# Partition sums by 32x32 block transposes on VectorE, a 129th column of ones, wider first scores, a last pass on three engines

## The chip, the cores and the metric

The kernel runs on one core of a Trainium2 chip. A core has a matrix engine (TensorE, PE in the profile), three engines for elementwise work (VectorE or DVE, ScalarE or ACT, GpSimd or POOL), and SyncE (SP), which here only issues transfers from memory. Each engine takes its instructions strictly in the order in which they stand in the program, and waits for the others by semaphores. The metric is the device time of one execution in microseconds, the median of the runs shown.

## The reference: what is computed

Two cross-attention layers over a batch of 8; all numbers are float32. x has 100 rows of 1024 per batch, ctx has 1444 rows of 512.

Layer 0, per batch:

```python
Q = x @ Wq + bq;  K = ctx @ Wk + bk;  V = ctx @ Wv + bv      # hidden size 1024
weights = softmax(Q @ K.T * 1024**-0.5, axis=-1)             # over the 1444 context rows
x = x + (weights @ V) @ Wo + bo
```

Layer 1, per batch, on that x, with weights of its own:

```python
q = x @ Wq + bq;  k = ctx @ Wk + bk;  v = ctx @ Wv + bv
w = softmax(q @ k.T * 1024**-0.5, axis=1)                    # over the 100 rows of x
y = w @ v + x
out = (y - mean(y)) * rsqrt(var(y) + 1e-6) * gamma + beta    # over the 1024 columns
```

In layer 0 a row of weights sums to 1. In layer 1 it does not: the softmax runs over the other axis. So w @ (ctx @ Wv + bv) needs, for each row of x, the sum of its weights over the 1444 context rows, times bv.

## The kernel before, in words

The kernel never forms K and V. It multiplies weight matrices with each other first: Wq times Wk transposed (tile `qk0`, later `qk1`) and Wv times Wo (`vo0`), then folds x into the first (`queries`, tiles `g0T` and `g1T`), so that scores are g times ctx, and then only needs ctx itself.

**Stages in the order of time.** 
1. `weight_products("qk0")`, then `weight_products("vo0")`: 1024 x 512 and 512 x 1024 products by Strassen's scheme in seven half products on TensorE (helper `half_product`, L124, bank names x, z, y, w). VectorE makes the sums of blocks (L135) and adds partial products (L247), ScalarE copies others out of PSUM (L242). `accumulate` (L264, L266) makes on VectorE the products of a bias with the rows of a weight matrix: for each of 8 row blocks, times a column of the bias, added up. What is left is a sum over the 128 partitions.
2. `totals` (L301) makes that sum: it transposes 128x128 pieces through TensorE with the identity (L307) and reduces them from PSUM on VectorE (L308). It does so for `u0`, `wqbk0`, `bvo`, later `u1` and `wqbk1`: 20 transposes before `queries(0)` and 12 after `qk1`; the sums for `c0` add 8 more (L400, L401).
3. `queries(0)`: again seven products (`seven_products`, banks g_x, g_z, g_y, g_w). `left_sums` and `right_sums` are on VectorE (L135), `put` copies a bank out on ScalarE with the bias u (L353), `add` adds a bank on VectorE (L358). The order of products is X, Z, Y, X, X, W, Y: the second and third X product add into the banks of the first, with a `put` of those banks before each. `T_[2]`, the right sums of the third X product, is the tile `g_t3`. Between these copies ScalarE adds `out_bias` to xT, row block by row block (L406), in place; each waits until nobody else reads that row block of the old xT.
4. `key_bias_sums` (L329, L331) on VectorE, then `weight_products("qk1")`.
5. `scores0` of batches 0 and 1 alone (L488, 4 rows of blocks times 11 pieces of 131 or 132 columns in 4 banks), then eight passes that interleave `weighted_rows` of batch b (L458) with `scores0` of batch b + 2, matmul by matmul. Softmax runs on ScalarE and VectorE, the transposition of the probabilities on VectorE in 32x32 blocks (L523). For batches 0 and 7 the first four pieces are transposed on TensorE instead (`first_transposed`).
6. `project0`, `queries(1)`, and the same two-deep scheme for layer 1: `scores1` (L603) for batch b + 2 beside `attend1` (L659) for batch b. `weight_sums` (L639 to L641) adds the weights of a batch over its 12 pieces on VectorE; `weight_totals` (L647, L649) finishes the sum by a transpose on TensorE and a reduce. The result `r` is used at L731.
7. `finish`, `project_last`, `normalise`: residual, statistics, normalisation, stores. For the last batch the last multiply-add is done in two halves on VectorE (L754), one stored by SyncE and one by ScalarE.

**What sets the order.** TensorE's order is as written (`manual_schedule`). The order on VectorE, ScalarE and GpSimd is chosen when the program is built, and so is the choice of a PSUM bank (6 in one pool, 2 in the other). SyncE issues loads as written, each as soon as its buffer is free. ctx passes through ten buffers of one size (`unit`); a pass takes eight of them, four for rows (`load_rows`, tiles c, L437 and L441) and four for columns (tiles cT, L418 or L426).

Of the kernel before, what the change touches and what calls it, by code (L numbers as in the profile page):

```python
# [30 lines left out]
P = 128  # L31
# [10 lines left out]
CUTS = [S * n // NP for n in range(NP + 1)]  # L42
QD = 32
# [10 lines left out]
def two_layer_cross_attention(ctx: ExitStack, tc: tile.TileContext, a: dict, out: bass.AP):  # L54
# [17 lines left out]
    def unit(name):  # L72
        return stream.tile([P, E + L], F32, tag="unit", name=name)
# [113 lines left out]
    def weight_products(name, left, right, l_width, r_width, scaled):  # L187
# [10 lines left out]
        if name == "qk0":  # L198
            for part in (slice(0, lh // 2), slice(lh // 2, lh)):
                nc.scalar.dma_start(out=units[0][:, part], in_=lsrc[:, 0, part])  # L200
            nc.sync.dma_start(out=units[0][:, l_width : l_width + rh], in_=rsrc[:, 0, :rh])
            for h in range(1, EC):
                nc.sync.dma_start(out=units[h][:, :lh], in_=lsrc[:, h, :lh])
                nc.sync.dma_start(out=units[h][:, l_width:], in_=rsrc[:, h, :])
                if h == 1:
                    nc.sync.dma_start(out=units[0][:, l_width + rh :], in_=rsrc[:, 0, rh:])
            for i in range(H):
                for h in (i, H + i):
                    nc.sync.dma_start(out=units[h][:, lh:l_width], in_=lsrc[:, h, lh:])
        else:  # L210
            for h in range(EC):
                nc.sync.dma_start(out=units[h][:, :l_width], in_=lsrc[:, h, :])
                nc.sync.dma_start(out=units[h][:, l_width:], in_=rsrc[:, h, :])
# [37 lines left out]
        def accumulate(side):  # L251
            for v, of in scaled:
                if of != side:
                    continue
                width = (l_width, r_width)[side]
                if width == E:
                    acc = row(f"{name}_{v}")
                else:
                    acc = work.tile([P, L], F32, tag="half", name=f"{name}_{v}", bufs=1)
                accs[v] = acc  # L260
                for h in range(EC):
                    src = units[h][:, :l_width] if side == 0 else units[h][:, l_width:]
                    if h == 0:
                        nc.vector.tensor_scalar(acc, src, cols[v][:, h : h + 1], None, ALU.mult)  # L264
                    else:
                        nc.vector.scalar_tensor_tensor(acc, src, cols[v][:, h : h + 1], acc, ALU.mult, ALU.add)  # L266
# [33 lines left out]

    def totals(name, acc, n):  # L301

        got = const.tile([P, n], F32, tag=name, name=name)
        for c in range(0, n, 4):
            ps = bank(f"{name}_{c}")
            for i in range(4):
                nc.tensor.transpose(ps[:, i * P : (i + 1) * P], acc[:, (c + i) * P : (c + i + 1) * P], ident)  # L307
            nc.vector.tensor_reduce(got[:, c : c + 4], ps.rearrange("p (c q) -> p c q", q=P), AX.X, ALU.add)  # L308
        return got

    def bias_product(layer):

        prod = small.tile([P, EC], F32, tag="bb", name=f"bb{layer}")
        nc.vector.tensor_tensor(prod, cols[f"L{layer}_xattn_bq"], cols[f"L{layer}_xattn_bk"], ALU.mult)
        part = small.tile([P, 1], F32, tag="bbs", name=f"bbs{layer}")
        nc.vector.tensor_reduce(part, prod, AX.X, ALU.add)
        ps = bank(f"bb_ps{layer}")
        nc.tensor.matmul(ps[:, 0:1], ones, part, start=True, stop=True)
        got = const.tile([P, 1], F32, tag=f"bqbk{layer}", name=f"bqbk{layer}")
        nc.vector.tensor_scalar(got, ps[:, 0:1], SCALE, None, ALU.mult)  # L320
        return got

    def key_bias_sums(name, t0, t1, wqbk):

        acc = work.tile([P, GT], F32, tag="kb", name=name, bufs=3)
        for k in range(EC):
            src = xT[:, k, t0:t1]
            if k == 0:
                nc.vector.tensor_scalar(acc, src, wqbk[:, k : k + 1], None, ALU.mult)  # L329
            else:  # L330
                nc.vector.scalar_tensor_tensor(acc, src, wqbk[:, k : k + 1], acc, ALU.mult, ALU.add)  # L331
        return acc
# [52 lines left out]
    bqbk0 = bias_product(0)  # L385
    bqbk1 = bias_product(1)
    wvo, (acc_o,) = weight_products("vo0", "L0_xattn_WvT", "L0_xattn_Wo", L, E, (("L0_xattn_bv", 1),))
    u0 = totals("u0", acc_u, LC)
    wqbk0 = totals("wqbk0", acc_c, EC)
    nc.vector.tensor_tensor(out_bias, out_bias, totals("bvo", acc_o, EC), ALU.add)  # L390
    gT = [queries(0, wqk0, u0), None]
# [4 lines left out]
    c0 = const.tile([T, B], F32, tag="c0", name="c0")  # L396
    for g in range(B // G):
        ps = bank(f"c0_ps{g}")
        for i in range(G):
            nc.tensor.transpose(ps[:T, i * P : (i + 1) * P], kb0[g][:, i * T : (i + 1) * T], ident)  # L400
        nc.vector.tensor_reduce(  # L401
            c0[:, g * G : (g + 1) * G], ps[:T].rearrange("p (b q) -> p b q", q=P), AX.X, ALU.add
        )
    nc.vector.tensor_scalar(c0, c0, SCALE, bqbk0[:T], ALU.mult, ALU.add)
# [24 lines left out]
    def load_rows(b):  # L429

        src = a["ctx_512"][b]
        for q in range(NQ):
            t = unit(f"c_{b}_{q}").rearrange("p (c l) -> p c l", c=CQ)
            n = CQ - (q == NQ - 1)

            rows = bass.AP(src.tensor, src.offset + q * QR * L, [[L, P], [MR * L, n], [1, L]])
            nc.sync.dma_start(out=t[:, :n, :], in_=rows)  # L437
            if n < CQ:
                m = (MC - 1) * MR
                for r0, r1 in ((0, 112), (112, MR + MX)):  # L440
                    nc.sync.dma_start(out=t[r0:r1, n, :], in_=src[m + r0 : m + r1, :])  # L441
            yield t
# [32 lines left out]
    def scores0(s, cT):  # L475
# [8 lines left out]
        banks = [bank(f"s0_{b}_{n}") for n in range(0, NP, PM)]  # L484
        for k in range(LC):
            for n in range(NP):
                o = CUTS[n // PM * PM]
                nc.tensor.matmul(  # L488
                    banks[n // PM][:T, CUTS[n] - o : CUTS[n + 1] - o],
                    q0[:, k, t0 : t0 + T],  # L490
                    cT[k][:, CUTS[n] : CUTS[n + 1]],
                    start=(k == 0 and n % PM == 0),
                    stop=(k == LC - 1),
                    skip_group_check=True,
                )
                if (k, n) != (LC - 1, NP - 1):
                    yield
        parts = small.tile([T, len(banks)], F32, tag="maxima", name=f"maxima_{b}")
        for n, ps in enumerate(banks):
            o, e = CUTS[n * PM], CUTS[min((n + 1) * PM, NP)]  # L500
            nc.scalar.activation(p[:, o:e], ps[:T, : e - o], AF.Identity, bias=c0[:, b : b + 1], scale=SCALE)  # L501
            nc.vector.tensor_reduce(parts[:, n : n + 1], p[:, o:e], AX.X, ALU.max)  # L502
# [73 lines left out]
    def key_bias1(g):  # L576

        acc = key_bias_sums(f"kb1_{g}", g * GT, (g + 1) * GT, wqbk1)
        ps = bank(f"c1_ps{g}")
        nc.tensor.matmul(ps[:, :GT], ones, acc, start=True, stop=True)  # L580
        c1 = work.tile([P, GT], F32, tag="kb", name=f"c1_{g}", bufs=3)
        nc.vector.tensor_scalar(c1, ps[:, :GT], SCALE, bqbk1, ALU.mult, ALU.add)
        return c1
# [67 lines left out]
    def attend1(s, c):  # L651

        b, w = s["b"], s["w"]
        ps = bank2(f"A1_{b}")
        for m in range(MC):
            r = held(m)
            for k in range(LC):
                part = slice(k * P, (k + 1) * P)
                nc.tensor.matmul(  # L659
                    ps[:T, part],  # L660
                    w[:r, m, :],
                    c[m // CQ][:r, m % CQ, part],
                    start=(m == 0 and k == 0),
# [3 lines left out]
                if (m, k) == (MC - 1, LC - 1):  # L667
                    s["A"] = work.tile([P, L], F32, tag="half", name=f"A1r_{b}", bufs=1)[:T]
                    nc.scalar.copy(s["A"], ps[:T, :])
# [69 lines left out]
    def normalise(s):  # L739
# [12 lines left out]
        for j in range(2):  # L752
            w = slice(j * E // 2, (j + 1) * E // 2)
            nc.vector.scalar_tensor_tensor(z[:, w], z[:, w], rstd, beta[:T, w], ALU.mult, ALU.add)  # L754
            (nc.scalar if j else nc.sync).dma_start(out=out[b][:, w], in_=z[:, w])
# [38 lines left out]
    run(scores0(batches[0], *loaded(load_features(0))))  # L794
    s0 = scores0(batches[1], *loaded(load_features(1)))
    for n in range(LC * NP):
        next(s0)
        if n == LC * NP - PT - 1:
# [32 lines left out]
    weight_sums(batches[0])  # L831
# [4 lines left out]
    for b in range(B):  # L836
# [7 lines left out]
        c, *cT = loaded(load_rows(b), *([load_columns(b + 2)] if nxt else []))  # L844
# [14 lines left out]
        weight_totals(batches[b])  # L859
        if b == B - 1:  # L860
            run(untransposed(batches[b]))
        if b + 1 < B:
# [34 lines left out]
```

## Time and profile before

| what | value |
|---|---|
| median of 3 runs | 653.84 us (652.96 to 654.14) |
| the profiled execution's own time | 653.41 us |
| its span, from its first to its last instruction | 651.6 us |
| TensorE busy | 641.9 us of the span |
| VectorE busy | 401.1 us |
| ScalarE busy | 128.2 us |
| mean granted clock of TensorE | 0.996 |

The lines of the profile are read like this. A timeline line has the start and the length in us, the engine, the line of the kernel, the operation, the tiles (written <- read) with their sizes, and how many instructions it merges. A float32 matmul of this kernel shows as two instructions, a transpose as one. In brackets stands how long the engine had been idle before it, and what ended that. A line of the waits has who waited for whom, the total in us, how often, and the longest. A window line has, for a stretch, each engine's busy time, TensorE's granted clock, the DMA share (the busy share of 16 DMA engines) and the rate. The matmul pipeline overlaps, so the start of the next line is a better measure of a group's cost than the length printed.

### The profile page before, as it was taken

To read this page: it belongs to the slowest core of one execution; us is meant where nothing else is said; L and a number is where in the kernel's file an instruction comes from. 1 tells how busy PE (TensorE), PEld (TensorE's weight loads), DVE (VectorE), ACT (ScalarE), POOL (GpSimd) and SP (SyncE) were. 2 spreads that over 40 slices of the span, in tenths; PEclk is the share of its full clock that TensorE was granted. 3 is DMA by queue.
4 is the path that set the end of the run, shared out by engine and by line. 5 is a ranking of instruction groups with operands and counts; after the bars stand their busy time and mean duration, and the time that the engine had idled before them with its cause. 6 is when DMAs were issued, how large, how long until landed. Compare 5 with 4: busy or idle time off the path is not lost.

```text
span 651.6 us, 10319 instructions
## 1 busy us (share of the span) xinstructions
PE 641.9 (99%) x4272; PEld 544.1 (84%) x4272; DVE 401.1 (62%) x764; ACT 128.2 (20%) x320; POOL 39.3 (6%) x44
## 2 busy tenths in 40 slices
PE   9999999999999999999999999999999999999994
PEld 7886445568899999999998555589999999999992
DVE  4979737996145775576662875268344433556984
ACT  1010010330203333312320000204232222310221
POOL 5000000000000000000000000000000000000763
PEclk9999999999999999999999999999999999999998
DMA  8937037000089788998999003029799998920122
GB/s 292 387 107 288 0 94 287 2 0 2 0 319 305 266 316 297 322 318 305 329 357 340 0 0 130 1 95 282 262 306 294 305 316 294 309 95 1 51 76 76
DMA packets 60236, 127.51 MB, mean 196 GB/s; under 512 B 3929, under 2 KB 22873, under 8 KB 60189
## 3 DMA queue, kind: packets, MB, share of 16 engines
q1 hardware_dynamic: 57742, 119.82, 53.9%
q0 software_dynamic: 2048, 6.56, 3.0%
q8 instruction: 33, 0.54, 0.3%
q10 hardware_dynamic: 398, 0.47, 0.2%
q14 instruction: 15, 0.11, 0.1%
HBM read 123.56 MB, written 3.28 MB: 195 GB/s over the span
## 4 chain that ended last, share of the span: by engine, by line
PE 58%; issue 35%; POOL 4%; DMA 1%; SPq 0%; POOLq 0%; ACT 0%; DVE 0%; DVEq 0%
PE A L458 12%; PE s L488 12%; PE qk_x L124 6%; PE qk_y L124 4%; PE vo_x L124 3%; PE o_x L124 3%; POOL z L749 3%; PE g_x L124 3%; PE qk_w L124 2%; PE qk_z L124 2%; PE vo_y L124 2%; PE g_y L124 2%; PE o_y L124 1%; PE vo_w L124 1%; PE vo_z L124 1%
## 5 line engine op out<-in xcount | busy, mean ns | idle before, releaser
L458 PE MATMUL A<-w,c 120*128 120x100 f32 x960 | 145.0, 267 | 0.0
L458 PEld LDWEIGHTS A<-w,c 120*128 120x128 f32 x960 | 130.1, 191 | 0.0
L603 PE MATMUL s<-g1T,cT 128*120 128x100 f32 (+1 forms) x768 | 123.2, 262 | 0.0
L488 PE MATMUL s<-cT,g0T 128*100 128x131 f32 (+1 forms) x704 | 119.5, 275 | 0.0
L659 PE MATMUL A<-c,w 120*100 120x128 f32 (+1 forms) x576 | 110.7, 273 | 0.0
L603 PEld LDWEIGHTS s<-g1T,cT 128*120 128x120 f32 (+1 forms) x768 | 105.2, 185 | 0.6 <-issue 0.3
L488 PEld LDWEIGHTS s<-cT,g0T 128*100 128x100 f32 x704 | 87.1, 167 | 0.0
L523 DVE STREAM_TRANSPOSE w<-prob 32x384 f32<-32x384 f32 (+1 forms) x128 | 68.6, 536 | 15.3 <-ACT prob L509 12.5
L659 PEld LDWEIGHTS A<-c,w 120*100 120x100 f32 (+1 forms) x576 | 74.0, 168 | 0.0
L623 ACT ACTIVATE w<-w,negmax 120x100 f32<-120x100 f32 (+1 forms) x96 | 35.1, 366 | 75.3 <-DVE negmax L621 75.3
L613 DVE SCALAR_TENSOR_TENSOR w<-s,c 120x400 f32<-120x400 f32 (+1 forms) x24 | 13.8, 573 | 41.7 <-PE s L603 41.7
L501 ACT ACTIVATE prob<-s,c 100x394 f32<-100x394 f32 (+2 forms) x32 | 17.8, 562 | 97.0 <-PE s L488 96.8
L124 PE MATMUL qk_x<-qk 128*128 128x256 f32 x128 | 29.3, 385 | 0.4 <-DMA qk<-in_L_xattn_WkT 0.4
L502 DVE TENSOR_REDUCE maxima<-prob 100x1 f32<-100x394 f32 (+2 forms) x32 | 16.2, 527 | 21.5 <-ACT prob L501 21.2
L124 PEld LDWEIGHTS qk_x<-qk 128*128 128x128 f32 x128 | 24.1, 193 | 5.1 <-issue 1.2
L626 DVE RECIPROCAL rtotal<-total 120x4 f32<-120x4 f32 (+1 forms) x24 | 4.2, 176 | 28.2 <-ACT w L623 28.2
L745 POOL TENSOR_TENSOR rstd<-rstd,mhalf 100x1 f32<-100x1 f32 x8 | 7.5, 934 | 216.5 <-DVE rstd L744 216.4
L545 DVE TENSOR_TENSOR xT<-xT,o_x 128x400 f32<-128x400 f32 (+1 forms) x24 | 13.7, 603 | 8.3 <-PE o_x L124 7.9
L818 POOL DMA_DIRECT2D prob<-in_L_xattn_beta x1 | 0.5, 546 | 296.9 <-DVE w L523 296.9
L623 ACT ACTIVATION_READ_ACCUMULATOR w<-w,negmax 120x1 f32 (+1 forms) x96 | 17.9, 187 | 0.0
L266 DVE SCALAR_TENSOR_TENSOR qk_L_xattn_bk<-qk,L_xattn_bk,qk_L_xattn_bk 128x1024 f32<-128x1024 f32 x14 | 17.8, 1274 | 0.0
L640 DVE TENSOR_REDUCE part<-w 120x100 f32<-120x1100 f32 x8 | 17.2, 2144 | 0.0
(204 smaller groups left out, 894.1 us busy)
## 6 DMA issues: line engine op xcount, KB each, us to landing
c<-in_ctx SPq DMA_DIRECT2D x48, 768.0 KB, 7.4
cT<-in_ctxT SPq DMA_DIRECT2D x32, 728.0 KB, 6.6
cT<-in_ctxT SPq DMA_DIRECT2D x32, 722.0 KB, 6.3
c<-in_ctx SPq DMA_DIRECT2D x16, 512.0 KB, 8.8
vo<-in_L_xattn_Wo SPq DMA_DIRECT2D x8, 512.0 KB, 7.1
qk<-in_L_xattn_WqT SPq DMA_DIRECT2D x8, 512.0 KB
qk<-in_L_xattn_WqT SPq DMA_DIRECT2D x15, 256.0 KB, 5.4
qk<-in_L_xattn_WkT SPq DMA_DIRECT2D x15, 256.0 KB, 6.3
```

Source lines behind the costliest of these rows:

```text
L124: nc.tensor.matmul(banks[n // per][:, n % per * width : (n % per + 1) * width], lhs[i][:, n * P : (n + 1) * P], rhs[i], start=(fresh and i ...
L266: nc.vector.scalar_tensor_tensor(acc, src, cols[v][:, h : h + 1], acc, ALU.mult, ALU.add)
L458: nc.tensor.matmul(ps[:, k * T : (k + 1) * T], c[m // CQ][:r, m % CQ, k * P : (k + 1) * P], w[:r, m, :], start=(m == 0 and k == 0), stop=( ...
L488: nc.tensor.matmul(banks[n // PM][:T, CUTS[n] - o : CUTS[n + 1] - o], q0[:, k, t0 : t0 + T], cT[k][:, CUTS[n] : CUTS[n + 1]], start=(k == ...
L501: nc.scalar.activation(p[:, o:e], ps[:T, : e - o], AF.Identity, bias=c0[:, b : b + 1], scale=SCALE)
L502: nc.vector.tensor_reduce(parts[:, n : n + 1], p[:, o:e], AX.X, ALU.max)
L523: nc.vector.transpose(blocks(w, r, m0 * T + q * QD, T, MC - m0), blocks(p, q, m0 * MR + r * QD, MR, MC - m0),)
L603: nc.tensor.matmul(ps[:r, (m - m0) * T : (m - m0 + 1) * T], cT[m // CQ][:, k, o : o + r], q1[:, k, t0 : t0 + T], start=(k == 0), stop=(k = ...
L623: nc.scalar.activation(w[:r, m, :], w[:r, m, :], AF.Exp, bias=negmax[:r, m : m + 1], accum_out=total[:r, m : m + 1])
L640: nc.vector.tensor_reduce(part[:MR], w[:MR, :last, :].rearrange("p c t -> p t c"), AX.X, ALU.add)
L659: nc.tensor.matmul(ps[:T, part], w[:r, m, :], c[m // CQ][:r, m % CQ, part], start=(m == 0 and k == 0), stop=(m == MC - 1), skip_group_chec ...
L749: nc.gpsimd.tensor_tensor(z, z, beta[:T], ALU.add)
```

## The change

1. **Sums over partitions.** `totals` no longer uses TensorE. It transposes the accumulator in 32x32 blocks in place on VectorE, reduces over 32 columns, and a new helper `quarters` brings the four partial sums together: 16 copies of 32 partitions by n columns between partition quarters, and one reduce of 4. The same for `c0`, for which each batch's piece is transposed and reduced for itself. The buffer of `key_bias_sums` grows by 28 columns that GpSimd sets to zero. The totals of `qk0` stand before `vo0` in the program, `queries(0)` before the total of `bvo`.
2. **Bias products** of both layers share one matmul of two columns.
3. **Weights' sums as a 129th column.** For layer 1's batches 0 to 5 the buffer of rows holds 513 words per context row, the last a one (set by GpSimd). The fourth matmul of `attend1` takes 129 columns, in a bank of its own from the pool of six; ScalarE copies 384 columns, 128 columns and the sum. `weight_sums` and `weight_totals` remain for batches 6 and 7. All ctx buffers become three words wider, and rows stand at a stride of 513 words in layer 0 too.
4. **First scores** of batches 0 and 1: 4 pieces of 361 columns, a bank each, in place of 11. The transposes of batch 0's probabilities stand two matmuls ahead of the end of batch 1's scores (four before).
5. **Last pass** of the last batch: 768 columns by VectorE, 256 by ScalarE and then GpSimd, stored by SyncE and ScalarE.

```diff
-        return stream.tile([P, E + L], F32, tag="unit", name=name)
+        return stream.tile([P, CQ * (L + 1)], F32, tag="unit", name=name)
...
+    def quarters(name, sums, n):
+        split = small.tile([P, EC, P // QD], F32, tag="split", name=f"{name}_split")[:, :n, :]
+        for q in range(P // QD):
+            for r in range(P // QD):
+                nc.vector.tensor_copy(split[q * QD : (q + 1) * QD, :, r], sums[r * QD : (r + 1) * QD, :, q])
+        got = const.tile([P, n], F32, tag=name, name=name)
+        nc.vector.tensor_reduce(got, split, AX.X, ALU.add)
+        return got
+
     def totals(name, acc, n):
-        got = const.tile([P, n], F32, tag=name, name=name)
-        for c in range(0, n, 4):
-            ps = bank(f"{name}_{c}")
-            for i in range(4):
-                nc.tensor.transpose(ps[:, i * P : (i + 1) * P], acc[:, (c + i) * P : (c + i + 1) * P], ident)
-            nc.vector.tensor_reduce(got[:, c : c + 4], ps.rearrange("p (c q) -> p c q", q=P), AX.X, ALU.add)
-        return got
+        nc.vector.transpose(acc, acc)
+        sums = small.tile([P, EC, P // QD], F32, tag="sums", name=f"{name}_sums")[:, :n, :]
+        nc.vector.tensor_reduce(sums, acc.rearrange("p (c q i) -> p c q i", q=P // QD, i=QD), AX.X, ALU.add)
+        return quarters(name, sums, n)
...
-        acc = work.tile([P, GT], F32, tag="kb", name=name, bufs=3)
+        acc = work.tile([P, GT + P - T], F32, tag="kb", name=name, bufs=3)
+        nc.gpsimd.memset(acc[:, GT:], 0.0)
...
-    bqbk0 = bias_product(0)
-    bqbk1 = bias_product(1)
-    wvo, (acc_o,) = weight_products("vo0", "L0_xattn_WvT", "L0_xattn_Wo", L, E, (("L0_xattn_bv", 1),))
+    bqbk0, bqbk1 = bias_products()
     u0 = totals("u0", acc_u, LC)
     wqbk0 = totals("wqbk0", acc_c, EC)
+    wvo, (acc_o,) = weight_products("vo0", "L0_xattn_WvT", "L0_xattn_Wo", L, E, (("L0_xattn_bv", 1),))
+    gT = [queries(0, wqk0, u0), None]
     nc.vector.tensor_tensor(out_bias, out_bias, totals("bvo", acc_o, EC), ALU.add)
-    gT = [queries(0, wqk0, u0), None]
...
+    sums = small.tile([P, EC, P // QD], F32, tag="sums", name="c0_sums")
     for g in range(B // G):
-        ps = bank(f"c0_ps{g}")
         for i in range(G):
-            nc.tensor.transpose(ps[:T, i * P : (i + 1) * P], kb0[g][:, i * T : (i + 1) * T], ident)
-        nc.vector.tensor_reduce(
-            c0[:, g * G : (g + 1) * G], ps[:T].rearrange("p (b q) -> p b q", q=P), AX.X, ALU.add
-        )
-    nc.vector.tensor_scalar(c0, c0, SCALE, bqbk0[:T], ALU.mult, ALU.add)
+            t = small.tile([P, P], F32, tag="kbT", name=f"kbT_{g}_{i}")
+            nc.vector.transpose(t, kb0[g][:, i * T : i * T + P])
+            nc.vector.tensor_reduce(
+                sums[:, g * G + i, :], t.rearrange("p (q j) -> p q j", j=QD), AX.X, ALU.add
+            )
+    c0 = quarters("c0", sums, B)
+    nc.vector.tensor_scalar(c0, c0, SCALE, bqbk0, ALU.mult, ALU.add)
...
-        banks = [bank(f"s0_{b}_{n}") for n in range(0, NP, PM)]
+        n_pieces, per = (NB, 1) if alone else (NP, PM)
+        cuts = [S * n // n_pieces for n in range(n_pieces + 1)]
+        banks = [bank(f"s0_{b}_{n}") for n in range(NB)]
...
+        whole, rest = bank2(f"A1_{b}"), bank(f"A1r_{b}")
+        o = (LC - 1) * P
         for m in range(MC):
             r = held(m)
             for k in range(LC):
-                part = slice(k * P, (k + 1) * P)
+                to = rest[:T, : P + 1] if k == LC - 1 else whole[:T, k * P : (k + 1) * P]
                 nc.tensor.matmul(
-                    ps[:T, part],
+                    to,
                     w[:r, m, :],
-                    c[m // CQ][:r, m % CQ, part],
-                    start=(m == 0 and k == 0),
+                    c[m // CQ][:r, m % CQ, k * P : (L + 1 if k == LC - 1 else (k + 1) * P)],
+                    start=(m == 0 and k in (0, LC - 1)),
...
-                    s["A"] = work.tile([P, L], F32, tag="half", name=f"A1r_{b}", bufs=1)[:T]
-                    nc.scalar.copy(s["A"], ps[:T, :])
+                    A = s["A"] = work.tile([P, L], F32, tag="half", name=f"A1q_{b}", bufs=1)[:T]
+                    nc.scalar.copy(A[:, :o], whole[:T, :o])
+                    nc.scalar.copy(A[:, o:], rest[:T, :P])
+                    s["r"] = small.tile([T, 1], F32, tag="r", name=f"r_{b}", bufs=6)
+                    nc.scalar.copy(s["r"], rest[:T, P : P + 1])
...
-        for j in range(2):
-            w = slice(j * E // 2, (j + 1) * E // 2)
-            nc.vector.scalar_tensor_tensor(z[:, w], z[:, w], rstd, beta[:T, w], ALU.mult, ALU.add)
-            (nc.scalar if j else nc.sync).dma_start(out=out[b][:, w], in_=z[:, w])
+        w, rest = slice(0, 3 * E // 4), slice(3 * E // 4, E)
+        nc.scalar.activation(z[:, rest], z[:, rest], AF.Copy, scale=rstd)
+        nc.gpsimd.tensor_tensor(z[:, rest], z[:, rest], beta[:T, rest], ALU.add)
+        nc.vector.scalar_tensor_tensor(z[:, w], z[:, w], rstd, beta[:T, w], ALU.mult, ALU.add)
+        nc.sync.dma_start(out=out[b][:, w], in_=z[:, w])
+        nc.scalar.dma_start(out=out[b][:, rest], in_=z[:, rest])
```

The built program shows what the scheduler makes of it. On VectorE the totals of `u0` and `wqbk0` follow straight on the sums of `qk0`; the work for `bvo`, `c0` and `qk1`'s biases comes before `T_[2]`. On ScalarE the first of the xT row blocks now stands between the two copies of the Y banks of `queries(0)`, and three more before the copies of the X banks (before: four, behind both copies of Y). `queries(0)` takes its X banks from those of vo_z.

## The prediction

> **What bounds the kernel now.** I read the page first, then the waits, then the timelines of TensorE, VectorE and ScalarE from 36 to 215 us.
>
> ```profile
> PE 641.9 (99%) x4272; PEld 544.1 (84%) x4272; DVE 401.1 (62%) x764; ACT 128.2 (20%) x320; POOL 39.3 (6%) x44
> ```
>
> TensorE is busy all the time up to its last matmul at 643.4 us. Its whole list of waits is two lines:
>
> ```profile
> PE warm L90 <- DVE mhalf L94: 1.1, 1, 1.1
> PE qk_x L124 <- DMA qk<-in_L_xattn_WkT: 0.4, 2, 0.2
> ```
>
> So work taken from TensorE is time, unless a wait appears. The timeline of TensorE shows what goes, and the place where a wait is nearest:
>
> ```profile
> 54.58 0.50 PE L318 MATMUL bb_ps<-bbs,ones 128*128 128x1 f32 x4
> 54.94 7.11 PE L124 MATMUL vo_x<-vo 128*128 128x512 f32 x16
> ...
> 103.18 0.60 PE L307 MATMUL u<-ident,qk_L_xattn_bq 128*128 128x128 f32 x4
> ...
> 105.36 5.54 PE L124 MATMUL g_x<-xT,qk 128*128 128x400 f32 x16
> ...
> 121.49 5.54 PE L124 MATMUL g_x<-g_t,g_s 128*128 128x400 f32 x16
> 127.04 5.64 PE L124 MATMUL g_x<-g_t,qk 128*128 128x400 f32 x16
> ...
> 191.69 1.04 PE L400 MATMUL c_ps<-ident,kb 128*100 128x128 f32 x8
> ...
> 193.87 19.11 PE L488 MATMUL s<-cT,g0T 128*100 128x131 f32 x168
> ```
>
> The product at 127.04 adds into banks that ScalarE must first have copied out. VectorE and ScalarE just before it:
>
> ```profile
> 39.66 1.27 DVE L135 TENSOR_TENSOR vo_s<-vo 128x512 f32<-128x512 f32 x2
> ...
> 86.13 2.03 DVE L135 TENSOR_TENSOR g_t<-xT 128x400 f32<-128x400 f32 x4 [8.99 <-PE vo_x L124]
> ...
> 121.40 2.02 DVE L135 TENSOR_TENSOR g_t<-xT 128x400 f32<-128x400 f32 x4
> ```
>
> ```profile
> 121.02 1.26 ACT L353 ACTIVATE g0T<-g_y,u 128x400 f32<-128x400 f32 x2 [9.48 <-PE g_y L124]
> 122.18 3.51 ACT L406 ACTIVATE xT<-xT,L_xattn_bo 128x800 f32<-128x800 f32 x4
> 126.39 1.26 ACT L353 ACTIVATE g0T<-g_x,u 128x400 f32<-128x400 f32 x2 [0.70 <-PE g_x L124]
> ```
>
> The four L406 write xT, and can start only when VectorE's last reads of those rows are done (the L135 at 121.40). The copies out (L353) stand behind them on ScalarE and had 0.70 us to spare. This is the one tight place.
>
> [...] This trace: sixteen 32x256 in 7.32 us (L523, from 208.71) and seven 32x384 in 4.14 us, so 0.458 and 0.59 us each, 0.19 us plus 1.035 ns per column. [...] (L390, 128x8: the next starts 0.08 us later; two L320 in 0.13). [...] L746 takes 1.27 us alone and 2.68 at 616.13 under GpSimd's L749.
>
> **The change, part by part.** TensorE:
> - Forty transposes go. Twenty before g_x: 105.36 - 103.18 = 2.18. Twenty after qk1: 193.87 - 191.69 = 2.18.
> - Two bias matmuls become one: half of 54.94 - 54.58, 0.18.
> - First scores: 88 matmuls took 214.07 - 193.87 - 0.35 (the transposes of prob between) = 19.85, or 0.2256 each. 32 of 361 columns at the 400-column rate (5.37 / 8 = 0.671, so 0.606): 19.38. Gain 0.47.
> - Six wsum transposes: 0.10 each between their start (471.76) and the next (471.86), 0.62.
> - 129th column: 72 matmuls x 1.68 ns, plus 0.12.
> Sum: -5.5 us.
>
> VectorE. By the program's order the totals of qk0 now stand straight behind the sums that end at 39.66, and VectorE then has no rest until the L135 of 121.40: its idle stretches (4.17 at 47.09, 8.99 at 86.13, 4.13 at 95.73) fill up. I sum its list from 39.66 to that instruction at steps from start to start: 30 of 128x512 at 0.604 (18.1); 32 of 256 at 0.335 (10.7); 10 of 400 at 0.485 (4.9); 14 scalar-multiply-adds of 1024 at 1.20 (16.8), 14 of 400 at 0.545 (7.6), 7 of 512 at 0.66 (4.6); 5 plain multiplies (2.4). New: transposes 3 x 1.25, 2 x 0.72, 8 x 0.325 (7.8); reduces 2 x 0.60, 2 x 1.2, 8 x 0.2 (5.2); 64 small copies at 0.072 (4.6); small ones and waits on their own results 0.7. Together 83.4, so 123.1, against 121.40 now. Landings don't hold it: the qk1 loads (issued 91.4 to 100.3) are read from 98 on, each some 7 us after its issue or later.
>
> Meanwhile TensorE wants to start the product of 127.04 at 127.04 - 2.18 - 0.18 = 124.7. ScalarE: first g_t done at 123.1 + 0.57 = 123.7; then, in its new order, xT (0.85), the second g_y copy (0.58), three xT (2.55), the copy out of g_x's first bank (0.66): 128.35. The new wait is 3.7 us. Not shown before: 32-element groups in a reduce. L640, with groups of 11, takes 2144 ns for 1100 elements, about 10 ns more a group; 128 groups of the new reduces would add 0 to 1.3. Small copies at 0.063 would take 0.6 off; fully serial ones (0.15 busy each) add 5.0. I take +0.5: wait 4.2, ends 2.6 and 9. Late next: W and the last g_y product, both of whose sums come 3 us ahead; nothing else until g1.
>
> Costed at nothing, with the cover: reduces and weight sums that leave VectorE (0.25 + 2.1 us a batch, under the matmuls). Two more ScalarE copies at a pass's end (0.8 us) before transposes that come 10 matmul pairs (4 us) later; the second bank is the longest free. GpSimd's 24 memsets wait for the same release as the loads; a cT load may start some 0.5 us later, against a lead of one pass (19.6 us) less 6 to 9 us of landing. Rows at a stride of 513 words: from 215 to 354 us the DMA share is 0.93 at 317 GB/s[...]. The transpose of batch 0's prob now has 8.5 instead of 9.0 us from its scores, of which 4.9 are needed.
>
> Last pass: after GpSimd's power at 646.42 two halves ended at 647.87. Now VectorE's 768 columns need 0.97 alone, 1.6 if GpSimd's 256 (a quarter of 2.36 = 0.6) shut it out; SP's issue (0.31) is shorter than ScalarE's (0.57), the piece is 300 and not 200 KB. -0.4 to +0.5, taken +0.1.
>
> Sum: -5.5 + 4.2 + 0.1 = -1.2 us. The profiled execution took 653.41 (span 651.6 and 1.8 around it): 652.2. The runs' median, 653.84, is 0.43 above it: 652.6, and for the skew to dearer small work I say 652.7.
>
> **Rivals.**
> - No wait: VectorE reaches the g_t in time, all 5.5 kept: 648.4. It needs 3.7 us less on VectorE than the rows give, nearly all of the new transposes or copies. Against it: ScalarE had only 0.70 us to spare.
> - Slower: the small copies don't overlap. At 0.15 each the wait is 8.7 and the time 653.84 - 5.5 + 8.7 + 0.1 = 657.1. It decides from 0.10 each on (wait over 5.4, no gain). For it: sixteen reads of a result just written. Against: L320 and L390.
> - DMA takes over: c rows more than 15% slower put the share over 1, and each of 12 passes with both loads grows by up to 0.5 us: up to 660 with the wait as forecast. Against: the cT pieces of the second layer, 1456 bytes[...], land 722 to 728 KB in 6.3 to 6.6 us, no slower per byte than c (768 KB in 7.4).
>
> **How the numbers follow.** What a measurement of this kernel can tell from no change is 0.2%, 1.3 us: 652.5 to 655.1. Chances: the forecast, wait 2.6 to 5.5, 651.0 to 653.9: 0.62, of which 0.33 lies under 652.5 and 0.29 within. No or little wait: 0.08, faster. Dearer small work, 653.9 to 657.5: 0.20, of which 0.08 within and 0.12 slower. DMA, ports or tail: 0.10, 0.09 slower. Faster 0.41, same 0.38, slower 0.21. The range 650.6 to 656.2 leaves out most of the second case and the far ends of the last two; the likeliest's own is 651.0 to 653.9.
>
> **What would show it.** TensorE's waits: one new line, the L124 of g_x on ScalarE (or, through it, VectorE's g_t), about 4 us near 124. g_x starts near 103.0, the product behind the wait near 128.9 (127.04 before), qk1's first near 145, the first scores near 193.5. VectorE without rest from 37 to 123; small copies at 0.07. Wrong if that wait is absent or over 5.5, if loads of c land later than 10 us, or if TensorE waits anywhere after 200 us.

## The result and the profile after

The changed kernel takes 659.98 us (median of 4 runs, 659.40 to 660.21), the kernel before 653.40 us in the same comparison. The ratio is 1.0099, with a 95% interval of 1.0081 to 1.0116: about 6.6 us slower. The prediction said 652.7 us, at most 656.2. The profiled execution of the changed kernel took 659.76 us, with a span of 657.6.

The waits of TensorE in the changed kernel (who waits for whom, us in total, how often, the longest) have the one new line that was forecast, at the forecast place, but twice as long:

```profile
PE g_x L124 <- ACT g0T L364: 8.5, 1, 8.5
PE warm L90 <- DVE mhalf L94: 1.1, 1, 1.1
PE qk_x L124 <- DMA qk<-in_L_xattn_WkT: 0.8, 1, 0.8
```

TensorE's timeline around it (start, length, engine, line, operation, tiles; in brackets the idle time before it):

```profile
102.75 5.54 PE L124 MATMUL g_x<-xT,qk 128*128 128x400 f32 x16
...
118.87 5.54 PE L124 MATMUL g_x<-g_t,g_s 128*128 128x400 f32 x16
132.91 8.06 PE L124 MATMUL g_x<-g_t,qk 128*128 128x400 f32 x16 [8.51 <-ACT g0T L364]
140.81 5.54 PE L124 MATMUL g_w<-g_t,qk 128*128 128x400 f32 x16
...
151.56 7.07 PE L124 MATMUL qk_x<-qk 128*128 128x256 f32 x32
...
199.98 18.41 PE L505 MATMUL s<-cT,g0T 128*100 128x361 f32 x60
```

The product behind the wait is eight matmuls (sixteen instructions) like its neighbours, and took 7.9 us from its start to the next start (132.91 to 140.81), not 5.5 as before (127.04 to 132.51). Busy time by window in the changed kernel shows why. The columns are the window, its length, the busy time of PE, PEld, DVE, ACT and POOL, the granted TensorE clock, the DMA share and the rate:

```profile
124.00:130.00 6.00, 0.41 (x2) 0.00 (x0) 5.85 (x19) 1.62 (x3) 0.00 (x0) 0.80 0.01 1
124.30:132.90 8.60, 0.11 (x1) 0.00 (x0) 8.46 (x24) 4.52 (x7) 0.00 (x0) 0.69 0.00 1
132.91:140.81 7.90, 7.89 (x16) 4.28 (x17) 7.60 (x31) 0.43 (x1) 0.00 (x0) 0.69 0.00 0
137.00:139.00 2.00, 2.00 (x6) 1.14 (x5) 1.89 (x8) 0.00 (x0) 0.00 (x0) 0.79 0.00 0
```

During the wait and the product behind it the clock is 0.69 on average: in finer windows 0.80 from 124 to 130, 0.50 from 130 to 137, 0.79 from 137 to 139, then 1.00. In the kernel before, the same product ran at 1.00. So the wait costs twice: 8.5 us of rest, and 2.4 us of slow work after it.

Comparing the starts of TensorE's stages, of before (the lines of the prediction) and of after, gives the whole account:

| from | to | before | after | difference | cause |
|---|---|---|---|---|---|
| span's start | first g_x product | 105.36 | 102.75 | -2.6 | transposes and a bias matmul gone (-2.4), the first products 0.2 earlier |
| first g_x product | third X product | 21.68 | 30.16 | +8.5 | the wait |
| third X product | first qk1 product | 16.22 | 18.65 | +2.4 | slow clock |
| first qk1 product | first scores | 50.61 | 48.42 | -2.2 | transposes gone |
| first scores | first pass | 20.20 | 19.81 | -0.4 | wider first scores |
| first pass | last matmul's end | 429.4 | 428.9 | -0.5 | sums as a 129th column |
| last matmul's end | span's end | 8.1 | 8.9 | +0.8 | last pass |

The differences add up to the span's 6.0 us; another 0.35 lies outside the span (659.76 - 657.6 = 2.16, against 1.81), for which I found no cause.

What made TensorE wait is on VectorE. Its timeline in the changed kernel, from the first totals to the sums that the third X product reads (the L135 of 127.78):

```profile
39.44 0.72 DVE L313 STREAM_TRANSPOSE qk_L_xattn_bq<-qk_L_xattn_bq 128x512 f32<-128x512 f32 x1
...
42.88 2.78 DVE L306 COPY u_split<-u_sums 32x4 f32<-32x4 f32 x16
...
85.47 2.85 DVE L306 COPY bvo_split<-bvo_sums 32x8 f32<-32x8 f32 x16
...
122.98 2.81 DVE L306 COPY c_split<-c_sums 32x8 f32<-32x8 f32 x16
...
127.78 2.03 DVE L135 TENSOR_TENSOR g_t<-xT 128x400 f32<-128x400 f32 x4
```

Sixteen copies take 2.8 us, so 0.175 each, where the prediction had 0.072. And ScalarE's timeline behind it:

```profile
128.38 0.96 ACT L418 ACTIVATE xT<-xT,L_xattn_bo 128x800 f32<-128x800 f32 x1 [9.39 <-DVE g_t L135]
129.25 0.58 ACT L364 ACTIVATE g0T<-g_y,u 128x400 f32<-128x400 f32 x1
129.73 2.65 ACT L418 ACTIVATE xT<-xT,L_xattn_bo 128x800 f32<-128x800 f32 x3
132.28 1.06 ACT L364 ACTIVATE g0T<-g_x,u 128x400 f32<-128x400 f32 x2
```

The copies of the X banks (the last line) had been possible since 124.3, when the product that fills them ended. They stand behind four additions to xT, the first of which waits for VectorE's late sums. That is the chain of the prediction; its first link was late.

### The profile page after: what moved, and what is told of

Read it like the earlier page. It is cut to its first block, busy times and chain, and to the rows that moved or that the text cites. A ratio compares the mean times of both kernels' runs of the same rounds, so it can differ in the third digit from the quotient of the medians.

```text
span 657.6 us, 10193 instructions
## 1 busy us (share of the span) xinstructions
PE 638.2 (97%) x4112; PEld 530.7 (81%) x4112; DVE 407.0 (62%) x856; ACT 129.6 (20%) x333; POOL 43.3 (7%) x73
## 4 chain that ended last, share of the span: by engine, by line
PE 80%; issue 11%; POOL 4%; DVE 2%; ACT 1%; DMA 1%; POOLq 0%; SPq 0%; DVEq 0%
PE A L473 12%; PE s L505 12%; PE s L620 10%; PE qk_x L124 6%; PE A L680 6%; PE g_x L124 5%; PE qk_y L124 4%; PE vo_x L124 3%; PE o_x L124 3%; POOL z L773 3%; PE g_y L124 2%; PE qk_w L124 2%; PE qk_z L124 2%; PE vo_y L124 2%; PE A1r L680 2%
## 5 line engine op out<-in xcount | busy, mean ns | idle before, releaser
L505 PE MATMUL s<-cT,g0T 128*100 128x131 f32 (+2 forms) x592 | 119.0, 296 | 0.0
L505 PEld LDWEIGHTS s<-cT,g0T 128*100 128x100 f32 x592 | 77.7, 167 | 8.4
L680 PE MATMUL A<-c,w 120*100 120x128 f32 (+1 forms) x432 | 83.0, 273 | 0.0
L680 PEld LDWEIGHTS A<-c,w 120*100 120x100 f32 (+1 forms) x432 | 55.5, 168 | 0.0
L518 ACT ACTIVATE prob<-s,c 100x394 f32<-100x394 f32 (+3 forms) x32 | 18.0, 563 | 94.1 <-PE s L505 93.9
L519 DVE TENSOR_REDUCE maxima<-prob 100x1 f32<-100x394 f32 (+3 forms) x32 | 16.3, 527 | 24.6 <-ACT prob L518 24.4
L680 PE MATMUL A1r<-c,w 120*100 120x129 f32 x144 | 27.8, 274 | 0.0
L124 PE MATMUL g_x<-g_t,qk 128*128 128x400 f32 x32 | 13.7, 591 | 8.5 <-ACT g0T L364 8.5
L124 PEld LDWEIGHTS g_x<-g_t,qk 128*128 128x128 f32 x32 | 7.0, 226 | 15.3 <-ACT g0T L364 9.1
L680 PEld LDWEIGHTS A1r<-c,w 120*100 120x100 f32 x144 | 18.5, 168 | 0.0
```

What stands on the lines that cost most here:

```text
L124: nc.tensor.matmul(banks[n // per][:, n % per * width : (n % per + 1) * width], lhs[i][:, n * P : (n + 1) * P], rhs[i], start=(fresh and i ...
L505: nc.tensor.matmul(banks[n // per][:T, cuts[n] - o : cuts[n + 1] - o], q0[:, k, t0 : t0 + T], cT[k][:, cuts[n] : cuts[n + 1]], start=(k == ...
L680: nc.tensor.matmul(to, w[:r, m, :], c[m // CQ][:r, m % CQ, k * P : (L + 1 if k == LC - 1 else (k + 1) * P)], start=(m == 0 and k in (0, LC ...
```

## The experiments

My theory after the result: (1) a small VectorE copy that changes its group of 32 partitions can't overlap with the one before, which makes 64 copies 6.6 us dearer than reckoned; (2) the wait that follows also costs TensorE its clock; (3) the last pass costs 0.8 us. The rivals are given in each expectation.

**The price of a copy, by kind.** Each of the six totals of the changed kernel gets its sixteen copies in a form of its own (`u0` keeps the old one). The totals of `wqbk0` and `wqbk1` then leave out most of what they should add; only the copies' time is read.

```diff
+                if name == "wqbk0":
+                    nc.vector.tensor_copy(split[one, :, r], sums[one, :, q])      # one = partitions 0 to 31
+                elif name == "wqbk1":
+                    nc.vector.tensor_copy(split[one, :, r], sums[of, :, q])
+                elif name == "bvo":
+                    nc.vector.tensor_copy(split[of, :, q], sums[to, :, r])
+                elif name == "u1":
+                    nc.vector.tensor_scalar(split[to, :, r], sums[of, :, q], 1.0, None, ALU.mult)
+                else:
+                    nc.vector.tensor_copy(split[to, :, r], sums[of, :, q])        # c0: split laid out without stride
```

> The six calls of `quarters` in the changed kernel, each with 16 small copies of another kind (the totals of wqbk0 and wqbk1 come out wrong: their copies all write partitions 0 to 31). Theory A: a small copy on VectorE is held until the one before has ended whenever its input or its output starts in another group of 32 partitions than the one before. Then u0 (as in the changed kernel), bvo (output group changes at each step, input group at every fourth), c0 (as u0, but written without stride), u1 (a multiply by 1 in place of a copy) and wqbk1 (input group alone changes) step at 0.17 us each, and wqbk0 (both always partitions 0 to 31) at 0.06 to 0.08. Rival B: 0.17 is the price of any such copy of 32 partitions; then wqbk0 steps at 0.17 too. Rival C: it is the stride of the output; then c0 alone is cheap. Rival D: it is the copy operation; then u1 alone is cheap. If only the input or only the output counted, bvo or wqbk1 would be cheap.

VectorE's timeline of this kernel:

```profile
42.38 2.79 DVE L321 COPY u_split<-u_sums 32x4 f32<-32x4 f32 x16
...
46.04 1.28 DVE L313 COPY wqbk_split<-wqbk_sums 32x8 f32<-32x8 f32 x16
...
83.31 2.85 DVE L317 COPY bvo_split<-bvo_sums 32x8 f32<-32x8 f32 x16
...
121.38 2.79 DVE L321 COPY c_split<-c_sums 32x8 f32<-32x8 f32 x16
...
125.40 2.10 DVE L319 TENSOR_SCALAR u_split<-u_sums 32x4 f32<-32x4 f32 x12
...
140.91 1.92 DVE L315 COPY wqbk_split<-wqbk_sums 32x8 f32<-32x8 f32 x10
```

Sixteen copies within one group of partitions take 1.28 us: the last one's own length taken off, (1.28 - 0.16) / 15 = 0.075 from start to start. Reckoned in the same way, all others take 0.175 (2.79), 0.18 (2.85), 0.175 (twelve in 2.10) and 0.195 (ten in 1.92). The length of one is the same in all, 0.15 to 0.17. So within a group the next copy starts while the last one is still under way, and otherwise it waits for its end. A change of the input's group alone is enough (wqbk1), and a change of the output's group with the input's kept for four copies is too (bvo). Stride, operation and width (4 or 8 columns) make no difference here. Theory A holds, its rivals fall.

**The same price, and the whole kernel's time.** All sixteen copies of each total are put on partitions 0 to 31. The totals leave out the other three quarters; the rest of the work is the same, with a small memset ahead of each group of copies.

```diff
+        nc.vector.memset(split, 0.0)
-                nc.vector.tensor_copy(split[q * QD : (q + 1) * QD, :, r], sums[r * QD : (r + 1) * QD, :, q])
+                nc.vector.tensor_copy(split[:QD, :, r], sums[:QD, :, q])
```

> The changed kernel, but all 16 small copies of each total read and write partitions 0 to 31 (behind a memset of the 128x32 buffer), so that none changes the group of partitions; the totals come out wrong. It has the price that the prediction assumed, 0.08 us a copy, with all else in place. Theory: 48 copies of 0.175 become 0.08 ahead of the third X product's sums, so VectorE reaches these at 123.3 us; ScalarE's copies of the X banks end near 127.9, TensorE waits 3.7 us (3 to 4.5) and its clock falls little: 653.2 - 5.5 + 3.7 + 1.1 (last pass and around the span) = 652.5 us (651.8 to 653.5). Rival (the wait has another cause than the copies' price): the wait stays over 7 us and the time over 657.

Measured: 649.74 us, ratio 0.9946 (0.9934 to 0.9959). TensorE's waits and VectorE's sums in this kernel:

```profile
PE qk_x L124 <- DMA qk<-in_L_xattn_WkT: 1.8, 1, 1.8
PE warm L90 <- DVE ones L87: 1.1, 1, 1.1
PE g_x L124 <- ACT g0T L365: 1.0, 1, 1.0
```

```profile
40.29 0.70 DVE L314 STREAM_TRANSPOSE qk_L_xattn_bq<-qk_L_xattn_bq 128x512 f32<-128x512 f32 x1
...
119.26 1.28 DVE L307 COPY c_split<-c_sums 32x8 f32<-32x8 f32 x16
...
121.62 1.98 DVE L135 TENSOR_TENSOR g_t<-xT 128x400 f32<-128x400 f32 x4
```

The direction is clear: with the copies' overlap restored and nearly all else kept, the wait falls from 8.5 to 1.0 us, and the kernel is faster than before the change. My number was 2.8 us too high. I had counted 48 copies ahead of the sums; there are 64 (u0, wqbk0, bvo, c0), which is 1.6 us of it. VectorE's list from its first transpose to the sums is 121.62 - 40.29 = 81.3 us, against 127.78 - 39.44 = 88.3: of these 7.0 us the copies are 64 x 0.10 = 6.4, and 0.2 are the last reduce and the scaling of c0, which now stand behind the sums. The last pass with its 0.8 us is still in this time; -5.5 + 1.0 + 0.8 + 0.1 outside the span gives 649.6 from 653.2.

**The clock.** The wait is left as it is, and TensorE gets idle work to do in it.

```diff
         put(0, 1, X)
+        if name == "g0":
+            for _ in range(32):
+                nc.tensor.matmul(idle[:, :P], ones, ones, start=True, stop=True)
```

> The changed kernel with 32 idle matmuls of ones with ones (about 7 us, results unused) ahead of the third X product of the first queries, where TensorE waits 8.5 us. Theory: the wait itself stays (the product starts at the same 132.9 us, since VectorE and ScalarE are unchanged), but the clock stays at 1.00 and the product takes 5.4 and not 7.9 us: 2.4 us less, 657.6 us (656.9 to 658.3). Rival (the slow product has another cause than TensorE's rest): 660, product still 7.9 us.

Measured: 657.13 us (656.95 to 657.45), ratio 1.0061 (1.0048 to 1.0074): 4.0 us over the kernel before, where the changed kernel is 6.6 over. TensorE's timeline:

```profile
123.77 7.31 PE L180 MATMUL idle<-ones 128*128 128x128 f32 x64
132.50 5.64 PE L124 MATMUL g_x<-g_t,qk 128*128 128x400 f32 x16 [1.43 <-ACT g0T L369]
137.98 5.54 PE L124 MATMUL g_w<-g_t,qk 128*128 128x400 f32 x16
```

The product starts within 0.4 us of where it did, and takes 5.5 us. The granted clock is 1.00 from 124 to 138 us. The slow product came from TensorE's rest alone. In the trace of the changed kernel the clock is halved from 127.6 us, 3.2 us after TensorE came to rest, to 137.8, which is 10.2 us. That covers 4.9 us of the product, half of which (2.4) is lost.

**ScalarE's place in the chain.** The additions to xT move to GpSimd; VectorE's order stays as it is.

```diff
-        nc.scalar.activation(xT[:, e, :], xT[:, e, :], AF.Identity, bias=out_bias[:, e : e + 1])
+        nc.gpsimd.tensor_scalar(xT[:, e, :], xT[:, e, :], out_bias[:, e : e + 1], None, ALU.add)
```

> The changed kernel with the eight additions of `out_bias` to xT on GpSimd instead of ScalarE; VectorE's order is unchanged. Theory (of the wait of 8.5 us, 4.0 are VectorE's late sums and 4.5 the four xT additions and the copies that ScalarE does in order behind them): ScalarE's copies of the X banks are done long before, TensorE now waits for the first of VectorE's sums itself, done near 128.4: wait 4.1, so 4.4 us less: 655.6 us if the clock falls as far as before (2.4), 653.2 if not at all; up to 1 us more where GpSimd slows VectorE's sums: 653.2 to 656.6. Rival (ScalarE's place in the chain costs nothing, the wait is VectorE's alone): 660, wait 8.5.

Measured: 655.62 us (654.72 to 656.41), ratio 1.0038 (1.0025 to 1.0052). TensorE's timeline and its first wait:

```profile
PE g_x L124 <- DVE g_t L135: 4.2, 1, 4.2
```

```profile
128.55 8.14 PE L124 MATMUL g_x<-g_t,qk 128*128 128x400 f32 x16 [4.17 <-DVE g_t L135]
136.52 5.54 PE L124 MATMUL g_w<-g_t,qk 128*128 128x400 f32 x16
```

As forecast: of the 8.5 us, 4.2 are VectorE's lateness and the rest is ScalarE's queue. The shorter wait loses the clock just as the long one did (7.97 us from start to start, 2.5 too many), whereas the wait of 1.0 us above lost nothing. The clock in this run, and the same product in the kernel with copies of each kind, where TensorE waits 8.7 us:

```profile
124.00:128.00 4.00, 0.38 (x2) 0.00 (x0) 3.84 (x16) 0.93 (x2) 0.00 (x0) 0.85 0.01 2
132.00:136.00 4.00, 4.00 (x11) 2.29 (x10) 4.00 (x7) 0.00 (x0) 4.00 (x2) 0.79 0.00 0
```

```profile
132.66 7.34 PE L124 MATMUL g_x<-g_t,qk 128*128 128x400 f32 x16 [8.66 <-ACT g0T L379]
139.84 5.54 PE L124 MATMUL g_w<-g_t,qk 128*128 128x400 f32 x16
```

In these three waits the loss does not grow with the length. Here the clock was halved at 126.8, after only 2.4 us of rest (TensorE worked until 124.4), was 0.50 from 128 to 132, and was back at 133.6, after 6.8 us. In the other kernel the product took 7.2 us, 1.7 too many. What sets the moment at which the clock falls and comes back isn't shown: this is read from three traces, and no run shifted one and the same wait.

**Part 1 alone undone.** The sums over partitions, those of `c0` too, return to the transposes on TensorE, and the totals to their old place in the program; the other four parts stay.

```diff
-        nc.vector.transpose(acc, acc)
...
-        return quarters(name, sums, n)
+        for c in range(0, n, 4):
...
+                nc.tensor.transpose(ps[:, i * P : (i + 1) * P], acc[:, (c + i) * P : (c + i + 1) * P], ident)
+            nc.vector.tensor_reduce(got[:, c : c + 4], ps.rearrange("p (c q) -> p c q", q=P), AX.X, ALU.add)
```

> The changed kernel with part 1 alone undone: the sums over partitions as before, by transposes on TensorE. Theory: the wait of 8.5 us and the slow clock behind it (2.4 us) are gone; TensorE keeps 0.18 + 0.47 + 0.50 = 1.15 of gains, the last pass costs 0.8 and the surroundings of the span 0.3 more: 653.4 - 1.15 + 1.1 = 653.4 us (652.7 to 654.2). Rival (one of the other parts costs the time): 656 or more.

Measured: 652.77 us (13 runs, 652.36 to 653.27), ratio 0.9994 (0.9986 to 1.0002). The only wait of TensorE left is that of the warm-up. So all of the loss, but for the last pass, sits in part 1. The other four parts together make no measurable difference: by the table TensorE gains 1.1 us from them and the last pass costs 0.8, and 0.4 was measured.

**Part 1 with one small matmul in place of sixteen copies.** The transposes and reduces on VectorE stay. The four partial sums are added on TensorE with a 0/1 matrix `spread` (ones where two partitions have the same place in their groups), which leaves each sum in all four groups; a 0/1 mask `own` and a reduce pick the right one.

```diff
-        for q in range(P // QD):
-            for r in range(P // QD):
-                nc.vector.tensor_copy(split[q * QD : (q + 1) * QD, :, r], sums[r * QD : (r + 1) * QD, :, q])
+        nc.tensor.matmul(ps[:, :nq], spread, sums.rearrange("p c q -> p (c q)"), start=True, stop=True)
+        nc.vector.tensor_tensor(
+            split,
+            ps[:, :nq].rearrange("p (c q) -> p c q", q=P // QD),
+            own.unsqueeze(1).to_broadcast([P, n, P // QD]),
+            ALU.mult,
+        )
```

> The changed kernel, but the four partial sums are brought together by one small TensorE matmul per total with a 0/1 matrix, a multiply by a 0/1 mask and a reduce, in place of 16 small copies. 64 copies leave VectorE before the third X product's sums. Theory (the small copies make VectorE late, and TensorE waits for it): no wait of TensorE on ScalarE, its clock never falls after the warm-up, TensorE's work is 5.5 us less five matmuls of about 0.15, so 4.8 less than before; the last pass costs 0.8 us more and what lies around the span 0.3 more, as in the changed kernel: 653.4 - 4.8 + 1.1 = 649.7 us (648.7 to 651). Rival (the time was lost elsewhere: transfers at the wider stride, ports, banks): a wait may go, but the time stays above 654.

Measured: 652.70 us (13 runs, 651.71 to 654.51), ratio 0.9995 (0.9986 to 1.0003), 3 us above the forecast and outside its range. The wait of the changed kernel is gone, and TensorE's waits show what took its place:

```profile
PE wqbk_ps L311 <- DVE c L428: 2.0, 1, 2.0
PE warm L90 <- DVE mhalf L100: 1.1, 1, 1.1
PE vo_x L130 <- DVE qk L253: 0.7, 1, 0.7
```

Two new waits give back 2.7 us: the totals of qk0, early in VectorE's order, delay the additions out of the banks that vo_x needs; and the last total's sums have to wait for one of two buffers, which is free only after the c0 matmul at the end of qk1. So I mended both; the edit is against the kernel just shown:

```diff
+    wvo, (acc_o,) = weight_products("vo0", "L0_xattn_WvT", "L0_xattn_Wo", L, E, (("L0_xattn_bv", 1),))
     u0 = totals("u0", acc_u, LC)
     wqbk0 = totals("wqbk0", acc_c, EC)
-    wvo, (acc_o,) = weight_products("vo0", "L0_xattn_WvT", "L0_xattn_Wo", L, E, (("L0_xattn_bv", 1),))
...
-        sums = small.tile([P, EC, P // QD], F32, tag="sums", name=f"{name}_sums")[:, :n, :]
+        sums = small.tile([P, EC, P // QD], F32, tag="sums", name=f"{name}_sums", bufs=3)[:, :n, :]
```

and put the last pass of the kernel before in the place of the new one.

> The kernel with the small TensorE matmul per total, with three edits against its two new waits (0.75 us of vo_x on VectorE's sums into qk, 2.0 us of the wqbk1 matmul on a buffer of sums): the totals of u0 and wqbk0 stand behind vo0 again, as before the change; three buffers of sums instead of two; and the last pass as before the change. Theory: no wait of TensorE is left after the first loads, so 4.8 us of TensorE's work are gone and nothing is given back: 653.2 - 4.8 = 648.4 us (647.7 to 649.5). Rival (the 2.7 us of waits only move to another place, since VectorE has 13 us more work before 130 us): 650.5 or more, with a wait of TensorE on VectorE or ScalarE.

Measured: 649.11 us (648.40 to 649.89), ratio 0.9938 (0.9924 to 0.9951), about 4.1 us faster than before. TensorE's waits are:

```profile
PE warm L90 <- DVE mhalf L100: 1.1, 1, 1.1
PE qk_y L130 <- DVE qk_s L141: 0.2, 1, 0.2
```

That is within the range forecast. This version beats both kernels, and keeps about 4 of the 5.5 us that the change took from TensorE.

**The last pass alone**, on the kernel before:

```diff
-        for j in range(2):
-            w = slice(j * E // 2, (j + 1) * E // 2)
-            nc.vector.scalar_tensor_tensor(z[:, w], z[:, w], rstd, beta[:T, w], ALU.mult, ALU.add)
-            (nc.scalar if j else nc.sync).dma_start(out=out[b][:, w], in_=z[:, w])
+        w, rest = slice(0, 3 * E // 4), slice(3 * E // 4, E)
+        nc.scalar.activation(z[:, rest], z[:, rest], AF.Copy, scale=rstd)
+        nc.gpsimd.tensor_tensor(z[:, rest], z[:, rest], beta[:T, rest], ALU.add)
...
```

> The kernel before with the new last pass of the last batch alone (768 columns on VectorE, 256 on ScalarE and then GpSimd). Theory (the trace of the changed kernel: from the end of GpSimd's power to the end of the span 5.97 us against 5.18): 0.8 us slower in the span, up to 0.3 more outside of it: 653.9 to 654.4 us. Rival (what the prediction's sum allowed, 0.4 less to 0.5 more): 652.8 to 653.7.

Measured: 654.13 us (14 runs) against 653.23, ratio 1.0015 (1.0007 to 1.0023), 0.9 us slower. The last steps of this kernel:

```profile
644.98 1.52 POOL L745 TENSOR_TENSOR rstd<-rstd,mhalf 100x1 f32<-100x1 f32 x1 [4.20 <-DVE rstd L744]
647.13 1.01 POOL L754 TENSOR_TENSOR z<-z,prob 100x256 f32<-100x256 f32 x1 [0.62 <-ACT z L753]
```

```profile
646.54 0.51 ACT L753 ACTIVATE z<-z,rstd 100x256 f32<-100x256 f32 x1 [9.09 <-POOL rstd L745]
648.17 0.56 ACTq L757 DMA_DIRECT2D out<-z  x1
```

```profile
646.54 1.02 DVE L755 SCALAR_TENSOR_TENSOR z<-z,rstd,prob 100x768 f32<-100x768 f32 x1 [0.46 <-POOL rstd L745]
```

And of the kernel before:

```profile
646.46 1.41 DVE L754 SCALAR_TENSOR_TENSOR z<-z,rstd,prob 100x512 f32<-100x512 f32 x2 [0.46 <-POOL rstd L745]
647.91 0.57 ACTq L755 DMA_DIRECT2D out<-z  x1
```

From the end of GpSimd's power (646.50) the second store's issue starts 1.67 us later; in the kernel before it was 1.49 (646.42 to 647.91). GpSimd's 256 columns take 1.01 us after ScalarE's 0.51, and so end later (648.14) than the two halves on VectorE did (647.87). VectorE's 768 columns took 1.02 us and were held up by nothing. GpSimd's addition began 0.43 us before their end and had 0.58 us left after it, which is a quarter of the 2.35 us of 1024 columns. So it looks as if GpSimd had waited for VectorE, and not the other way round as the prediction allowed for; no run shows it by itself.

The other 0.6 to 0.7 us come after the issue: 3.8 us from its end to the span's end here, 3.1 before. The packets in the traces show where they go. The second store's data began to move 1.77 us after the start of its issue here and 1.14 us before, and then took 1.1 to 1.2 us in both. The first store, of 300 KB in place of 200, was moving until 650.62 here and until 649.42 before; the second one's last packet ended last, at 651.05 and 650.22. Whether the smaller store waited for the larger one was not tested.

## Why the prediction was wrong, step by step

**The step that failed** is the price of the small copies: "64 small copies at 0.072 (4.6)". They cost 0.175 each, 11.2 us. The rest of that sum was 1.6 us too high: the transposes took 6.5 and not 7.8 us (0.63, 1.12 to 1.16 and 0.22 for 512, 1024 and 128 columns), the reduces 4.9 and not 5.2. So VectorE's list took 88.3 us, not 83.4, and reached the sums at 127.8, not at 123.1.

The rows that I took as the nearest (L320 and L390) don't change the group of 32 partitions; the sixteen copies go through all pairs of groups, so each one changes at least one, in whatever order they stand, and the runs price that: 0.175 us a copy with a change, 0.075 without. The trace of before may have had it in a row that I did use: the 32x32 transposes of L523 move blocks between groups, and their fixed part was 0.19 us. The new transposes, which stay in place, fit a fixed part of 0.08 (0.22 for 128 columns, 0.63 for 512), a difference of 0.11, about that of the two kinds of copies (0.10). I read 0.19 as what a transpose costs; that the change of group is in it was not tested by itself.

**The chain behind it** was right: 4.64 us from the first sum to the free bank forecast, 128.38 to 132.91 = 4.53 measured. The place, the direction and the releaser of the wait were right. The case that came true is the slower rival, "the small copies don't overlap", and its wait, 8.7, was met within 0.2 (8.5). That it was met so closely is luck: the copies cost 1.6 us more than the 0.15 each of that case, and the transposes and reduces 1.6 us less than my sum. I gave dearer small work 0.20 of chance, 0.12 of it on the slower side, on two rows of the wrong kind.

**What that rival's own time lacked.** It said 657.1; measured were 659.98. A term was missing from every case: the clock. I priced a wait of TensorE as its length, while the one of 4.2 us in the GpSimd experiment already cost 2.5 more. The forecast wait of 4.2 could have cost as much. With 2.4 for the clock, 0.7 more for the last pass and 0.35 outside the span, less 0.2 for the shorter wait, 657.1 becomes 660.3. It was built on 653.84 us for the kernel before; on the 653.40 of the comparison it is 659.9.

**TensorE's gains** of 5.5 us came to 2.4 + 2.2 + 0.4 + 0.5 = 5.5. Each term was met within 0.1.

**The last pass**: +0.1 forecast, with +0.5 as its end; 0.8 in the trace and 0.9 in its own experiment. The sum feared that GpSimd would hold up VectorE's piece, which did not happen. It had no term for the chain that did end last, ScalarE's 0.51 and then GpSimd's 1.01 (0.6 in the sum, and beside VectorE's work), nor for the later start of the second store's data, which is the larger part.

**Costed at nothing, and rightly so**: no wait of TensorE after 200 us, in any version. Loads of c land in 8.1 us (7.4 before), under the 10 that I named as the limit, so "DMA takes over" did not happen. That the wider stride made them slower isn't shown: in the run with the new last pass alone, at the old stride, the same loads landed in 9.3 us. The DMA share in the passes of layer 0 is 0.92 at 316 GB/s (215 to 354 us), against 0.93 at 317 before: it did not rise.

**The wait's lower end**, 2.6 us, was too high as well: with the copies at the assumed price the wait is 1.0 and the kernel takes 649.7. What made my sum too long there is the 1.6 us of transposes and reduces above, the 0.5 that I had added for the reduces' groups, 0.58 of ScalarE's chain, since in that kernel both copies of the Y banks stand ahead of the additions to xT, and 0.2 of c0 behind the sums; 0.3 stay open. Had a copy cost what I assumed, my forecast would still have been off, by 3 us to the other side.

## What to carry to other kernels

Before a VectorE instruction gets a price, look at where it and its neighbour start: here a chain of short copies that hops between groups of 32 partitions cost 0.175 us for each, about its full length, instead of 0.075, and sixteen such hops could be one matmul with a 0/1 matrix. Price a wait of a TensorE that never rests as its length plus the slow clock behind it (here 2.5, 2.4 and 1.7 us more for 4.2, 8.5 and 8.7 us of rest, nothing for 1.0). And when work leaves the bounding engine, ask in which queue it now stands ahead of what that engine needs next: with some 5 us taken from TensorE in both kernels, the price of the work that replaced it, its order and the last pass decided between +6.6 and -4.1 us.

## What the runs showed of the hardware

- A VectorE copy of 32x8 elements lasts 0.15 to 0.17 us either way; from start to start it is 0.075 us within one group of 32 partitions, and 0.175 to 0.195 as soon as the group of the input or of the output changes.
- TensorE's clock fell to half during waits of 4.2 and 8.5 us, after 2.4 and 3.2 us of rest, and stayed there for 6.8 and 10.2 us, into the next product, which lost 2.5 and 2.4 us. The product behind a wait of 8.7 us lost 1.7, the one behind a wait of 1.0 us nothing. Idle matmuls in the wait of 8.5 us kept the clock at 1.00.
- GpSimd's addition of two 100x256 tiles took 1.01 us while VectorE worked in its first 0.43 us; one of 100x1024 took 2.35.
